# The layer-norm output of two graph-attention layers, moved from sixteen ScalarE operations to three GpSimd passes

## The chip, the cores and the metric

The kernel runs on one core of one Trainium2 chip. The metric is the device time of one execution in microseconds (us). One core has five engines that matter here, each with its own in-order queue of instructions: TensorE (PE in the profile, with its weight loads shown apart as PEld), VectorE (DVE), ScalarE (ACT), GpSimd (POOL), and SyncE (SP), which issues the DMAs.

## The reference

Four graph layers follow each other on `x` of shape 8 x 2048 x 64 (batch, nodes, features). All share one 2048 x 2048 adjacency matrix. After each layer comes a residual layer norm, cut here to what matters:

```
def _layernorm(x): m = mean(x); v = var(x); return (x - m) / sqrt(v + 1e-5)   # over 64 features
x = _layernorm(x + L0(x, adj))   # attention: softmax over neighbours, then elu; inner norm of h
x = _layernorm(x + L1(x, adj))   # attention, elu
x = _layernorm(x + L2(x, adj))   # attention, relu
x = _layernorm(x + L3(x, adj))   # a softmax per feature over the neighbours
```

Written with the statistics of a row, a norm's output is `o * rs + nm`, with `rs = 1/sqrt(var + eps)` and `nm = -mean * rs`, one value of each per node. This last step of the norms after layers 0 and 1 is what the change concerns.

## The kernel before

**Units.** A unit is one layer of one batch element. `todo` fixes their order: layer 0 of batches 0 to 3 (units 0 to 3), layer 1 of the same (4 to 7), layer 0 of batches 4 to 7 (8 to 11), layer 1 of these (12 to 15), and layer 2 of batches 0 to 7 (16 to 23). Layer 3 is a long series of matmuls that begins beside the units of layer 2 and goes on after the last one.

**Steps.** A unit has K = 16 steps, one for each block of 128 neighbours. In a step, `weights` makes a 128 x 2048 tile `w` on VectorE (maximum of a row term `r`, held in PSUM, with a column term, times the edge mask). In layer 2 only, `exponential` then takes the exponential of `w` on ScalarE. `products` multiplies `w` into the sums `acc` on TensorE. Four buffers hold `w`. At the end of a unit TensorE writes the next unit's row term `r` (`spread`, four matmuls `r<-row,ones`), which has to wait until VectorE has read the old one for the last time; VectorE then waits for the new `r`.

**Background streams.** All other work is written as Python generators which the main loop advances by one step after each step's products (`bg.step()`). `yield n` lets n steps go by before the generator's next piece is issued. So the generators and their yields set, at build time, the place of each background instruction in each engine's queue; `tc.keep_in_program_order` keeps that order. Waits on the chip are for data only: an instruction that is reached before its input is there holds its engine's queue.

**The streams around the change.** After a unit's last step a chain starts: `finish(u)` (transposes the sums, divides, adds the residual, normalizes), two steps of pause, then `scores(layer+1, b)`, which transposes the new `x` on TensorE (`p_xT...v<-ident,x`) and derives the next layer's scores. `features0(b)` prepares layer 0 of the later batches. In `finish` for layers 0 and 1:

- `side_stats` computes the row sums on GpSimd by repeated halving (`sq_x`, `st_x`), ScalarE squares the row (`sq_x<-o`), and GpSimd ends with a power (`st_x<-isw_x,mhalf`) and the two columns `rs` and `nm` (both in `st_x`).
- Line 1145: sixteen ScalarE operations, one for each block of 64 features, write `x<-o,st_x`. After each four of them comes `yield 1`.
- `xn.settle()`: a tile of `Rows` with `unit=True` keeps a column of ones in front of each row's 64 features, which overwrites the place where the last feature of the block before would lie. GpSimd first copies those last features to the end of the tile (`x<-x`, 128 x 16) and then sets the ones (`x<-`, memset). `Rows.parts` describes the resulting layout: features 0 to 62 in place, feature 63 at the end of the tile.

Others on GpSimd in these units are `hb` and `eh` (residual and elu), `pv` (values times their column factor, read by the next unit's products), `tree` (a sum over rows that TensorE reads for `p_mean`), `rT` (the row term, split in three) and `y`.

`now[1]` is the number of the unit whose steps are being issued when a line of a generator runs. A unit's `finish` lies in later units: its output is written one or two units after its last step.

Of the kernel before, what the change touches and what calls it, by code (L numbers as in the profile page):

```python
# [14 lines left out]
AF = mybir.ActivationFunctionType  # L15
ALU = mybir.AluOpType
# [34 lines left out]
def gnn4_kernel(ctx: ExitStack, tc: tile.TileContext, t, out):  # L51
# [3 lines left out]
    K = N // P  # L55
# [51 lines left out]
    class Banks:  # L107
# [4 lines left out]
        pool = None  # L112
# [28 lines left out]
    pe, dve, act, pool = (InOrder(e) for e in (nc.tensor, nc.vector, nc.scalar, nc.gpsimd))  # L141

    def psum(name):
        return pm.tile([P, 512], F32, tag="pm", name=name)

    def bc_f(v, n=K, f=F):
        return v[:, :, None].to_broadcast([P, n, f])

    def bc_k(v, n=K, f=F):
        return v[:, None, :].to_broadcast([P, n, f])  # L150
# [241 lines left out]
    for layer in range(3):  # L392
        rs = early.tile([P, F1], F32, tag="rs_w", name=f"rs_{layer}")
# [126 lines left out]
    def side_stats(y, name, st=None):  # L520

        centered = st is not None
        if not centered:
            st = small.tile([P, 2, K], F32, tag="st", name=f"st_{name}", bufs=4)
            yield from sq_slots.take()
            sq = tmp.tile([P, K, F], F32, tag="sq", name=f"sq_{name}")
            halved(st[:, 0], sq, y)
            yield 2
            act.activation(sq, y, AF.Square)
            yield 1  # L530
        else:
            sq = y
        s1, s2 = st[:, 0], st[:, 1]
        halved(s2, sq, sq)
        sq_slots.give()
        w = small.tile([P, 2, K], F32, tag="isw", name=f"isw_{name}", bufs=4)
        var, q = w[:, 0], w[:, 1]
        pool.tensor_scalar(var, s2, 1.0 / F, LN_EPS, ALU.mult, ALU.add)
        if not centered:
            pool.tensor_scalar(q, s1, 1.0 / F, None, ALU.mult)  # L540
            pool.tensor_tensor(s1, q, q, ALU.mult)
            pool.tensor_tensor(var, var, s1, ALU.subtract)
        pool.tensor_tensor(s2, var, mhalf, ALU.pow)
        if not centered:
            pool.tensor_scalar(q, q, -1.0, None, ALU.mult)
            pool.tensor_tensor(s1, q, s2, ALU.mult)
        yield 4 if now[0] < 2 else 2
        return s1, s2

    def stats(y, n, name):  # L550

        st = small.tile([P, 2, n], F32, tag="st", name=f"st_{name}", bufs=4)
        yield from sq_slots.take()
        sq = tmp.tile([P, n, F], F32, tag="sq", name=f"sq_{name}")
        act.activation(sq, y, AF.Square)
        dve.tensor_reduce(st[:, 0], y, AX.X, ALU.add)
        yield 2 if now[0] < 2 else 1
        dve.tensor_reduce(st[:, 1], sq, AX.X, ALU.add)
        sq_slots.give()
        yield from inv_std(st, n, name)  # L560
        return st[:, 0], st[:, 1]
# [490 lines left out]
    def finish(u):  # L1052
        layer, b = u.layer, u.b
        yield from oT_slots.take()
        oT = tmp.tile([P, 2, 512], F32, tag="oT", name=f"oT_{u.n}")
        for c in range(2):
            act.copy(oT[:, c], u.acc[c])
        if layer == 0:
            hb = early.tile([P, K, F], F32, tag="hb", name=f"hb_{u.n}", bufs=1)
            for sl, y in V[0, b].parts:  # L1060
                pool.tensor_tensor(
                    hb[:, :, sl], y, bc_k(gamma[:, sl], K, y.shape[2]), ALU.mult
                )
        yield 1
        yield from o_slots.take()
        o = tmp.tile([P, K, F], F32, tag="o", name=f"o_{u.n}", bufs=2)
        o5 = o.rearrange("p (c h s) f -> p c s h f", c=2, h=2)
        done = 0
        while done < 4:
            width = Banks.width()  # L1070
            ps = []
            yield from pm_slots.take(width)
            for i in range(done, min(done + width, 4)):
                c, s0 = i // 2, 2 * (i % 2)
                p = psum(f"p_o_{u.n}_{c}_{s0}")
                for s in range(2):
                    k = s0 + s
                    pe.matmul(
                        p[:, s * 2 * F1 : (s + 1) * 2 * F1],
                        lhsT=oT[:, c, k * P : (k + 1) * P],  # L1080
                        rhs=RH[layer].rearrange("p h f -> p (h f)"),
                        start=True,
                        stop=True,
                    )
                ps.append((c, s0, p))
            done += width
            if done >= 4:
                oT_slots.give()
            yield 2 if width == 2 else 1
            for c, s0, p in ps:  # L1090
                p4 = p[:, : 4 * F1].rearrange("p (s h f) -> p s h f", s=2, h=2)
                den = small.tile([P, 2, 2], F32, tag="den", name=f"den_{u.n}_{c}_{s0}")
                dve.reciprocal(den, p4[:, :, :, F])
                if layer == 2:
                    dve.tensor_tensor(
                        o5[:, c, s0 : s0 + 2],
                        p4[:, :, :, :F],
                        den[:, :, :, None].to_broadcast([P, 2, 2, F]),
                        ALU.mult,
                    )  # L1100
                    continue
                for s in range(2):
                    for h in range(2):
                        act.activation(
                            o5[:, c, s0 + s, h],
                            p4[:, s, h, :F],
                            AF.Copy,
                            scale=den[:, s, h : h + 1],
                        )
            pm_slots.give(width)  # L1110
        if layer == 2:
            for sl, x in x_cur[b].parts:
                dve.scalar_tensor_tensor(o[:, :, sl], o[:, :, sl], 0.0, x, ALU.max, ALU.add)
            yield 1
        else:
            yield 1
            if layer == 0:
                pool.tensor_tensor(o, o, hb, ALU.add)
                yield 2

            yield from e_slots.take()
            e = tmp.tile([P, K, F], F32, tag="e", name=f"eh_{u.n}")
            act.activation(e, o, AF.Relu, scale=-1.0)
            act.activation(e, e, AF.Exp, scale=-1.0)
            yield 1
            for sl, x in x_cur[b].parts:
                pool.tensor_tensor(
                    e[:, :, sl], e[:, :, sl], x, ALU.add
                )
            act.activation(o, o, AF.Relu)  # L1130
            yield 1
            pool.tensor_tensor(o, o, e, ALU.add)
            e_slots.give()
            yield 2
        if now[0] < 3:
            nm, rs = yield from side_stats(o, f"x_{u.n}")
        else:
            nm, rs = yield from stats(o, K, f"x_{u.n}")
        xn = Rows(x_cur[b].t, layer < 2)
        if layer == 2:  # L1140
            dve.tensor_tensor(o, o, bc_f(rs), ALU.mult)
            dve.tensor_tensor(xn.v, o, bc_f(nm), ALU.add)
        else:
            yield 1
            for k in range(K):
                act.activation(
                    xn.block(k), o[:, k], AF.Identity, scale=rs[:, k : k + 1], bias=nm[:, k : k + 1]
                )
                if k % 4 == 3:
                    yield 1  # L1150
            xn.settle()
        o_slots.give()
        x_cur[b] = xn
        V[layer + 1, b] = xn
        if layer < 2:
            yield 1
# [7 lines left out]
    now = [0, 0, 0]  # L1164
# [273 lines left out]
    for n, (layer, b) in enumerate(todo):  # L1438
# [10 lines left out]
        for jb in range(K):  # L1449
# [12 lines left out]
            if jb == K - 1:  # L1462
                end = [lambda u=u: finish(u)]
                if layer < 2:
                    end += [2 if now[0] < 2 else 1, lambda layer=layer, b=b: scores(layer + 1, b)]
                else:
                    end += [1, lambda b=b: l3_features(b)]
                if layer == 1 and b % NB == NB - 1:
                    end += [lambda b=b: group(b // NB)]
                bg.add(chain(*end), begun=True)  # L1470
            elif not done and jb >= 10 and ready(*nxt):
                prepare(*nxt)
                prepared.add(n + 1)
                done = True
# [524 lines left out]
```

## Time and profile before

| | |
|---|---|
| median of 3 runs | 1397.81 us (1397.5 to 1398.58) |
| profiled execution | 1401.63 us, of which span 1399.8 us |
| PE busy | 1220.0 us (87% of the span) |
| DVE busy | 1208.8 us (86%) |
| ACT busy | 821.6 us (59%) |
| POOL busy | 770.2 us (55%) |
| `x<-o,st_x` on ACT | 256 instructions, 91.5 us busy |

The span is that of the profiled execution from its first to its last instruction. Busy times count the time in which an engine has at least one instruction running; matmuls overlap each other, so a PE that shows 96% can still be waiting in part. All instructions carry the line of a helper (L80), so groups are told apart by the names of their tiles, with buffer numbers left out: `x<-o,st_x` reads `o` and `st_x` and writes `x`.

### The profile page before, as it was taken

To read this page: it belongs to the slowest core of one execution; us is meant where nothing else is said; L and a number is where in the kernel's file an instruction comes from. 1 tells how busy PE (TensorE), PEld (TensorE's weight loads), DVE (VectorE), ACT (ScalarE), POOL (GpSimd) and SP (SyncE) were. 2 spreads that over 40 slices of the span, in tenths; PEclk is the share of its full clock that TensorE was granted. 3 is DMA by queue.
4 is the path that set the end of the run, shared out by engine and by line. 5 is a ranking of instruction groups with operands and counts; after the bars stand their busy time and mean duration, and the time that the engine had idled before them with its cause. 6 is when DMAs were issued, how large, how long until landed. Compare 5 with 4: busy or idle time off the path is not lost.

```text
span 1399.8 us, 19531 instructions
## 1 busy us (share of the span) xinstructions
PE 1220.0 (87%) x7169; PEld 624.2 (45%) x7169; DVE 1208.8 (86%) x1108; ACT 821.6 (59%) x1593; POOL 770.2 (55%) x1075
## 2 busy tenths in 40 slices
PE   3699888999898988999997879799989999976995
PEld 3333233333343333333332324256645565666995
DVE  3889889999997999889998888998879798877876
ACT  3444543666646753555547996868666758664432
POOL 1666776546765663645542342443555564776664
PEclk8699999999999999999999988999999899998998
DMA  8640000000000221222101000034543444511111
GB/s 291 228 95 1 1 2 1 1 2 1 3 1 1 91 76 47 78 74 93 32 1 39 1 15 1 22 94 129 146 122 92 127 119 138 160 28 33 35 38 34
DMA packets 112010, 87.24 MB, mean 62 GB/s; under 512 B 57917, under 2 KB 90845, under 8 KB 110882
## 3 DMA queue, kind: packets, MB, share of 16 engines
q1 hardware_dynamic: 111538, 85.79, 20.9%
q8 instruction: 59, 0.97, 0.3%
q14 instruction: 45, 0.37, 0.1%
q10 hardware_dynamic: 368, 0.12, 0.0%
HBM read 60.40 MB, written 25.45 MB: 61 GB/s over the span
## 4 chain that ended last, share of the span: by engine, by line
PE 49%; DVE 24%; ACT 11%; issue 7%; POOL 6%; DMA 2%; SPq 1%; ACTq 0%; DVEq 0%; POOLq 0%
PE acc L80 26%; DVE w L80 16%; PE p_l L80 14%; ACT w L80 2%; PE p_o L80 2%; ACT x L80 2%; DVE o L80 1%; PE r L80 1%; PE p_s L80 1%; POOL sq_x L80 1%; DMA raw<-in_adjT_dram 1%; DVE nd L80 1%; POOL st_x L80 1%; DVE edge L80 1%; ACT y L80 1%
## 5 line engine op out<-in xcount | busy, mean ns | idle before, releaser
L80 DVE SCALAR_TENSOR_TENSOR w<-r,se,edge 128x2048 f32<-128x2048 f32 (+1 forms) x270 | 552.9, 2102 | 30.9 <-PE r L80 22.6
L80 PE MATMUL acc<-w,pv 128*64 128x512 f32 x2048 | 494.1, 615 | 53.0 <-DVE w L80 39.4
L80 DVE SCALAR_TENSOR_TENSOR w<-r,lo_g,edge 128x2048 f32<-128x2048 f32 (+1 forms) x144 | 297.8, 2096 | 26.0 <-PE r L80 12.4
L80 ACT ACTIVATE w<-w,down_g 128x2048 f32<-128x2048 f32 (+1 forms) x144 | 256.8, 1808 | 64.6 <-DVE w L80 57.4
L80 PEld LDWEIGHTS p_l<-v,mask 128*128 128x128 f32 x2048 | 256.3, 196 | 61.8 <-issue 48.5
L80 PE MATMUL p_l<-v,mask 128*128 128x256 f32 x2048 | 271.1, 291 | 10.6 <-POOL mask L80 7.0
L80 PE MATMUL acc<-w,x 128*64 128x512 f32 x1024 | 261.8, 640 | 19.2 <-ACT w L80 16.3
L80 PEld LDWEIGHTS acc<-w,pv 128*64 128x64 f32 x2048 | 132.6, 139 | 307.6 <-issue 182.4
L80 POOL TENSOR_TENSOR sq_x<-sq_x 128x32 f32<-128x32 f32 (+4 forms) x207 | 110.1, 532 | 63.8 <-ACT sq_x L80 49.3
L80 PEld LDWEIGHTS acc<-w,x 128*64 128x64 f32 x1024 | 66.5, 143 | 138.9 <-issue 86.6
L80 ACT ACTIVATE x<-o,st_x 128x64 f32<-128x64 f32 x256 | 91.5, 445 | 13.2 <-POOL st_x L80 13.2
L80 ACT ACTIVATE nd<-p_l,empty 128x256 f32<-128x256 f32 x64 | 30.2, 471 | 109.1 <-PE p_l L80 109.1
L80 ACT ACTIVATE o<-p_o,den 128x64 f32<-128x64 f32 x256 | 55.8, 323 | 47.0 <-DVE den L80 47.0
L80 PE MATMUL p_o<-rh,oT 128*128 128x130 f32 x384 | 61.9, 298 | 24.4 <-DVE o L80 6.7
L80 PEld LDWEIGHTS p_o<-rh,oT 128*128 128x128 f32 x384 | 50.2, 197 | 58.3 <-issue 32.3
L80 ACT COPY oT<-acc 128x512 f32<-128x512 f32 x48 | 25.7, 587 | 80.8 <-PE acc L80 80.8
L80 POOL TENSOR_TENSOR st_x<-isw_x,mhalf 128x16 f32<-128x16 f32 x24 | 70.5, 2938 | 1.9
L80 POOL TENSOR_TENSOR eh<-eh,x 128x1024 f32<-128x1024 f32 (+2 forms) x24 | 36.5, 1532 | 47.0 <-ACT eh L80 47.0
L80 DVE RECIPROCAL nd<-nd 128x256 f32<-128x256 f32 x32 | 55.7, 1742 | 0.0
L80 POOL TENSOR_TENSOR d<-x,wa_bc 128x1024 f32<-128x1024 f32 x8 | 19.0, 2379 | 66.5 <-DVE x L80 66.5
L80 POOL TENSOR_TENSOR sq_x<-o 128x512 f32<-128x512 f32 x23 | 29.3, 1273 | 34.6 <-DVE o L80 34.1
L80 ACT ACTIVATE xs<-x,nodes 128x64 f32<-128x64 f32 x128 | 44.7, 434 | 3.2 <-PE p_xT L80 3.2
(258 smaller groups left out, 1523.5 us busy)
## 6 DMA issues: line engine op xcount, KB each, us to landing
mask<-mask_d SPq DMA_DIRECT2D x132, 256.0 KB
mask_d<-mf SPq DMA_DIRECT2D x32, 512.0 KB
raw<-in_adjT_dram SPq DMA_DIRECT2D x8, 1024.0 KB
raw<-in_adjT_dram SPq DMA_DIRECT2D x16, 512.0 KB
x<-in_x_dram SPq DMA_DIRECT2D x8, 512.0 KB
x_d<-x SPq DMA_DIRECT2D x8, 512.0 KB
e<-x_d SPq DMA_DIRECT2D x64, 64.0 KB
out_dram<-o SPq DMA_DIRECT2D x64, 64.0 KB
```

Of the source, the lines that this page charges most:

```text
L80: ins = f(*args, **kwargs)
```

## The change

Where `now[1]` is 4 or more, the sixteen ScalarE operations and `settle` are replaced. GpSimd multiplies the whole 128 x 16 x 64 tile `o` by `rs`, broadcast along the features, in place; adds `nm` for the 63 features of each row that lie in place (128 x 16 x 63); adds it for the last features (128 x 16) into the end of the tile; and sets the ones. Four yields of one step each become one of two steps. Below 4 the code is as it was.

```
         else:
             yield 1
-            for k in range(K):
-                act.activation(
-                    xn.block(k), o[:, k], AF.Identity, scale=rs[:, k : k + 1], bias=nm[:, k : k + 1]
-                )
-                if k % 4 == 3:
-                    yield 1
-            xn.settle()
+            if now[1] < 4:
+                for k in range(K):
+                    act.activation(
+                        xn.block(k),
+                        o[:, k],
+                        AF.Identity,
+                        scale=rs[:, k : k + 1],
+                        bias=nm[:, k : k + 1],
+                    )
+                    if k % 4 == 3:
+                        yield 1
+                xn.settle()
+            else:
+                pool.tensor_tensor(o, o, bc_f(rs), ALU.mult)
+                for sl, x in xn.parts:
+                    pool.tensor_tensor(x, o[:, :, sl], bc_f(nm, K, x.shape[2]), ALU.add)
+                pool.memset(xn.v[:, :, 0:1], 1.0)
+                yield 2
         o_slots.give()
```

## The prediction, made before the changed kernel had run

> **What bounds the kernel now.** I began with the page's engine totals and its 40 slices, to see which engine is full where.
>
> ```profile
> PE 1220.0 (87%) x7169; PEld 624.2 (45%) x7169; DVE 1208.8 (86%) x1108; ACT 821.6 (59%) x1593; POOL 770.2 (55%) x1075
> PE   3699888999898988999997879799989999976995
> DVE  3889889999997999889998888998879798877876
> ACT  3444543666646753555547996868666758664432
> POOL 1666776546765663645542342443555564776664
> ```
>
> A slice is 35 us. DVE and PE are at 8 or 9 nearly everywhere; ACT is half busy, but reaches 9 in the two slices from 735 to 805 us. Which of these stages the change lies in needs times by unit. I take a unit's end at the last of its four `acc<-emptyT` matmuls. By that, units 4 to 7 run from 236 to 402 us, 8 to 15 to 744, unit 16 (the first of layer 2) to 792.8 and unit 17 to 845.1. The view of windows gives for these stretches, and for units 6 and 7 alone, the length and then the busy time of PE, PEld, DVE, ACT and POOL:
>
> ```profile
> 236.00:402.00 166.00, 154.88 (x782) 61.76 (x780) 154.82 (x111) 101.55 (x328) 103.73 (x159) 1.00 0.01 2
> 402.00:744.00 342.00, 311.90 (x1735) 122.46 (x1731) 317.08 (x234) 180.28 (x496) 189.51 (x279) 0.98 0.16 51
> 319.30:401.70 82.40, 77.60 (x395) 31.30 (x393) 77.61 (x58) 50.13 (x162) 60.06 (x96) 1.00 0.01 2
> 744.40:792.80 48.40, 38.16 (x180) 13.75 (x178) 39.36 (x26) 47.04 (x69) 15.89 (x25) 0.96 0.08 28
> 792.80:845.10 52.30, 41.73 (x189) 14.69 (x187) 47.35 (x48) 47.21 (x53) 17.13 (x24) 0.90 0.03 10
> ```
>
> In units 4 to 15 DVE is busy 472 of 508 us and PE 467: those two set the pace, and ACT (55%) does not. In unit 16 ACT is busy 47.04 of 48.40 us and is the bound, since every step there also takes an exponential on it. In unit 17 ACT and DVE are level at 90%. So I read the waits of DVE in both stretches (engine, what waited and for what: us in total, times, longest), first 236 to 744.4, then unit 16:
>
> ```profile
> DVE w L80 <- PE r L80: 23.0, 12, 3.2
> DVE den L80 <- PE p_o L80: 4.7, 3, 3.5
> DVE mean L80 <- ACT mean L80: 3.9, 2, 3.1
> ...
> DVE w L80 <- ACT eh L80: 2.7, 1, 2.7
> DVE w L80 <- PE r L80: 2.3, 1, 2.3
> DVE w L80 <- ACT w L80: 1.8, 1, 1.8
> DVE w L80 <- PE acc L80: 1.6, 1, 1.6
> ```
>
> In the first stretch nearly all waiting is for `r` at a unit's end; its shortest case is 1.11 us, so 13.3 of the 23.0 us are there anyhow. ACT appears with 3.9 us. The timeline of ACT says why, in unit 8: it stood 8.46 us at the first `x<-o,st_x`, and what was queued behind it (`mean`, `o`) came late to PE and DVE.
>
> ```profile
> 419.28 1.44 ACT L80 ACTIVATE x<-o,st_x 128x64 f32<-128x64 f32 x4 [8.46 <-POOL st_x L80]
> ```
>
> In unit 16, 2.7 + 1.8 + 1.6 = 6.1 us of DVE's waits come from a late ACT: the exponentials are late, so PE is late, so no `w` buffer is free.
>
> **What the Trainium skill says.** "GPSIMD Engine Reference", 3.1, gives 4497 ns for a float32 tensor_tensor add of 2048 elements per partition; half of it, 2.25 us, is an estimate for 1024. The trace agrees: 1.90 us for `pv<-x,se`, up to 2.38. The same page, 1, says that GpSimd's SBUF interfaces are shared with VectorE, with contention for DVE instructions of two SBUF inputs. `w<-r,se,edge` has one tensor in PSUM and one in SBUF, and shows none: I split it and its counterpart of layer 2, in single instructions of 128 x 2048, by overlap with POOL: the 84 with under 5% overlap and the 70 with 90% or more both average 2337 ns. "ScalarE: Activation LUTs", What ACT_TABLE_LOAD costs, gives 186 ns + 0.833 ns an element + 93 ns for each pointer operand, with 93 ns of overlap back to back: 425 ns here, or 332 in a row. The trace has 445 as the mean and 357 in a row (91.5 us / 256).
>
> **The change part by part.** The groups kept apart by shape:
>
> ```profile
> L80 ACT ACTIVATE x<-o,st_x 128x64 f32<-128x64 f32 x256 | 91.5, 445 | 13.2 <-POOL st_x L80 13.2
> L80 POOL TENSOR_TENSOR pv<-x,se 128x1024 f32<-128x1024 f32 x8 | 15.2, 1899 | 0.0
> L80 POOL TENSOR_TENSOR eh<-eh,x 128x1008 f32<-128x1008 f32 x8 | 15.9, 1993 | 33.6 <-ACT eh L80 33.6
> ```
>
> *How often.* The order of instructions of both built programs (no times) shows 32 of the 256 ScalarE operations left. `finish` lags: the outputs of units 0 and 1 are written while `now[1]` is 2 and 3, that of unit 2 in unit 4. So 14 of 16 outputs change, among them those of units 14 and 15, written in units 16 and 17.
>
> *Removed from ACT.* 14 x 16 operations, 14 x 5.7 us = 80 us busy. In units 4 to 15 this lies beside DVE and PE and is worth only the waits above. In unit 16 it is on the path.
>
> *Added to POOL.* Per output: the multiply by a broadcast column like `pv` (1.90; 2.38 at the upper end, as `d<-x,wa_bc`), the add of 1008 like `eh` (1.99; 2.34 as `hb`), 0.23 for 16 elements, less the 0.20 copy; the memset stays. That is 3.9 to 4.7 us, I take 4.2; times 14, 59 us. DVE, PE and ACT work hides it where POOL has room: 73% busy in units 6 and 7 becomes 83%.
>
> *Moved.* The passes follow `st_x` in POOL's own queue, so POOL itself waits for nothing new. Behind them come `pv`, `tree`, `rT`, `sq_x` of other streams, each later by up to 4.2 us. The next reader, PE's `p_xT...v`, comes five steps (some 12 us) after the passes are issued, two steps (4.8 us) earlier than before against `st_x`. I compared, for each of the 14 outputs, the time `st_x` was ready plus 4.5 us with the time at which PE came to a place two steps earlier: the slack is 11.8 to 34.7 us. I cost this wait at nothing; if that cover were gone, PE would stand in front of its `acc` matmuls. DMAs are the same in number; the `row` loads move with their streams.
>
> *PE's background.* Transposes just ahead of `r` (steps 13 and 14) delay it. In the new order they leave step 14 in units 7, 8 and 15 (before: 2.56, 3.05, 2.56 us of wait, after some 1.1 to 1.5: -4), and small pieces come in at units 9, 10, 12 and 13 (+1.5). PE has the same sum of work, so part of it is late elsewhere.
>
> *The sum.* Units 4 to 15: order at `r` -2.5 (of at most -9.7), the wait for `mean` -3.9, less crowding at `den` in unit 12 -0.6 (of 5.7), new waits behind a fuller POOL +3: together -4. Unit 16: ACT 47.0 - 5.8 = 41.3 us, DVE 39.4 plus 1.1 at `r`; I put the unit at 42.9, so -5.5 (between -2 and -7.9). Unit 17: DVE 47.35 busy and 5 us of waits, half of which hang on ACT: -2.5 (between 0 and -4.5). From step 11 of unit 18 on, all engines' orders are equal to before, so the rest is shifted. Sum -12. The profiled execution (1401.6 us, span 1399.8) lies 3.8 us above the median; I take the 12 us off the median: **1385.8 us**.
>
> **The rivals.**
>
> *Only layer 2 gains.* PE is 92% busy in units 4 to 15, so a transpose taken from a boundary delays another step. For it: the same PE work; against it: the 3.9 us behind the ACT wait have a cause that goes. -4 to -8: 1390 to 1394.
>
> *Nothing measurable.* In unit 16 PE and DVE are within 3 us of the relieved ACT and their mutual waits take its place: -2, 1396. Against it: 6.1 us of DVE's waits there are named.
>
> *Slower: POOL becomes the late one.* Its queue is in order, and PE waits for `pv` (slack 3.0 us at unit 7's start) and `tree` (1.5 us at 482 us). If POOL's backlog when the passes are issued exceeds the smallest slack of 11.8 us, the products PE needs come late by up to 4.2 us, once a unit: 12 x 4.2 = 50 us at most, half of it likely, less 8 from layer 2: about +17, 1415. For it: POOL's 83% in units 6 and 7; against it: in units 4 to 15 POOL stood idle for 31 us waiting for ACT's `x`, which goes.
>
> *More than planned.* All boundary waits at their floor and units 16 and 17 at DVE's own time: -9.7 - 3.9 - 7.9 - 4.5 = -26: 1372.
>
> *The change does less than it says* is excluded by the count; it does more (14 outputs, not 12).
>
> **How the numbers follow.** Forecast (-8 to -18) 0.50; only layer 2, 0.20; more than planned 0.09; nothing 0.09; slower by POOL 0.12. About 0.2% (2.8 us) is what a measurement of this kernel can tell from no change. Faster by more 0.79, within 0.09, slower 0.12. The range 1375 to 1397 takes in the bounds of units 16 and 17 and both smaller rivals, and leaves out the slower case and the end of the larger gain, together about 0.2.
>
> **What would show it.** ACT loses some 80 us busy and POOL gains some 59; POOL shows 128 x 1024 and 128 x 1008 passes of 1.9 to 2.4 us; unit 16 is near 43 us with ACT below 97%, unit 17 near 50; DVE no longer waits for `mean` in unit 8. It is wrong if PE waits for POOL's `x`, `pv` or `tree` by more than a few us, if the waits at `r` sum to over 23 us, or if unit 16 keeps its 48 us.

## The result, and the profile after

The changed kernel takes 1389.16 us in the median of 4 runs (1386.13 to 1391.82), beside 1398.19 us for the kernel before on the same chip: a ratio of 0.9934 with a 95% interval of 0.9907 to 0.9961, so 9 us faster. Run again later on another chip (19 runs), it had 0.9948 (0.9933 to 0.9964). The forecast was 1385.8 us.

The profiled execution took 1391.82 us, its span 1390.0 us, which is 9.8 us less than before. The page's engine totals and four of its rows of slices:

```profile
PE 1220.5 (88%) x7169; PEld 623.5 (45%) x7169; DVE 1214.1 (87%) x1108; ACT 751.3 (54%) x1369; POOL 817.7 (59%) x1103
...
PE   3689898999898979999997879799989899976996
...
DVE  3889889999999999889999899998879798877876
ACT  4444543446245544343436987867666768564432
POOL 1566777558668686756743543343646564676665
```

ACT lost 70.3 us and POOL gained 47.5 us. The work went where the diff says. DVE's number of instructions is the same (1108), yet it is busy 5.3 us longer: nothing in the diff touches DVE, so this is the first sign of a cost that the prediction did not have. The groups kept apart by shape:

```profile
L80 POOL TENSOR_TENSOR o<-o,st_x 128x1024 f32<-128x1024 f32 x14 | 26.6, 1900 | 0.0
L80 POOL TENSOR_TENSOR x<-o,st_x 128x1008 f32<-128x1008 f32 x14 | 26.3, 1876 | 1.1
...
L80 ACT ACTIVATE x<-o,st_x 128x64 f32<-128x64 f32 x32 | 11.6, 448 | 2.1 <-POOL st_x L80 2.1
...
L80 POOL TENSOR_TENSOR x<-o,st_x 128x16 f32<-128x16 f32 x14 | 3.3, 234 | 0.0
```

Fourteen outputs changed, and one costs 1.90 + 1.88 + 0.23 = 4.0 us of POOL. The view of windows for the stretches that were shown of before (units 4 to 7, 8 to 15, 6 and 7, 16, 17; length, then busy time of PE, PEld, DVE, ACT, POOL):

```profile
235.30:404.70 169.40, 156.73 (x772) 61.16 (x770) 159.36 (x110) 78.89 (x253) 110.00 (x152) 0.98 0.01 2
404.70:741.40 336.70, 311.73 (x1750) 122.12 (x1748) 315.25 (x235) 141.88 (x381) 229.72 (x313) 0.98 0.16 51
321.30:404.70 83.40, 77.44 (x379) 29.63 (x377) 78.71 (x56) 37.83 (x115) 57.44 (x83) 0.98 0.01 2
741.40:786.70 45.30, 36.25 (x184) 13.71 (x182) 40.43 (x27) 43.12 (x52) 17.62 (x27) 1.00 0.09 30
786.70:838.40 51.70, 41.37 (x189) 15.42 (x187) 47.98 (x56) 41.86 (x37) 19.96 (x26) 0.87 0.03 10
```

Measured by the exact ends of the units (the table further down), units 4 to 7 became 3.7 us longer, units 8 to 15 5.9 us shorter, unit 16 3.1 us and unit 17 0.6 us shorter. Unit 18, for which no gain was expected, lost 2.7 us (57.5 to 54.8), which is about what DVE's two waits for `den` there became shorter (1.96 + 1.85 us before, 0.54 + 0.41 after). DVE's waits (us in total, times, longest) in units 4 to 15, and then in unit 16:

```profile
DVE w L80 <- PE r L80: 23.4, 12, 2.8
DVE den L80 <- PE p_o L80: 3.0, 3, 1.8
DVE s_top L80 <- ACT s L80: 2.8, 2, 1.9
...
DVE w L80 <- PE acc L80: 3.5, 3, 1.7
DVE w L80 <- PE r L80: 1.3, 1, 1.3
```

The 3.9 us behind ACT's `mean` are gone. The waits for `r` did not shrink: 23.4 us against 23.0. What DVE lost instead is not in this view at all, since the profile counts it as busy. I looked for it by comparing each small DVE instruction with the shortest of its own kind, and found instructions of 0.2 us that last up to 2.3 us. The timeline of unit 5 (start, duration, engine, operation) has one:

```profile
288.29 0.20 DVE L80 TENSOR_TENSOR s<-h,st_h 128x32 f32<-128x32 f32 x1
288.31 2.08 POOL L80 TENSOR_TENSOR x<-o,st_x 128x1008 f32<-128x1008 f32 x2
288.53 1.74 DVE L80 TENSOR_TENSOR s<-s,s_off 128x32 f32<-128x32 f32 x1
...
290.30 0.43 ACT L80 ACTIVATE se<-s 128x16 f32<-128x16 f32 x3 [6.09 <-DVE s L80]
290.30 0.19 DVE L80 TENSOR_REDUCE s_top<-s 128x1 f32<-128x32 f32 x1
```

`s<-h,st_h` began just before the new pass and took 0.20 us. `s<-s,s_off`, of the same size, began after it and ended only when the pass over 1008 elements had (the timeline shows it with the short one behind it; alone it ran to 290.21). ACT, which needs `s` for `se`, stood 6.09 us; some 1.5 of these are the hold. Such excess over the shortest of a kind, counted where it is more than 0.25 us, sums to 15.2 us before and 20.3 us after between 236 and 845 us; of the latter 5.4 us lie under the new passes.

### The profile page after: what moved, and what is told of

It is laid out like the page before. It is cut to its first block, busy times and chain, and to the rows that moved or that the text cites. A ratio compares the mean times of both kernels' runs of the same rounds, so it can differ in the third digit from the quotient of the medians.

```text
span 1390.0 us, 19341 instructions
## 1 busy us (share of the span) xinstructions
PE 1220.5 (88%) x7169; PEld 623.5 (45%) x7169; DVE 1214.1 (87%) x1108; ACT 751.3 (54%) x1369; POOL 817.7 (59%) x1103
## 4 chain that ended last, share of the span: by engine, by line
PE 29%; DVE 15%; ACT 5%; issue 4%; POOL 2%; POOLq 0%; DVEq 0%; ACTq 0%
PE p_l L80 14%; PE acc L80 12%; DVE w L80 8%; DVE o L80 2%; ACT w L80 1%; PE p_o L80 1%; DVE nd L80 1%; DVE x L80 1%; ACT sp L80 1%; DVE fs L80 1%; PE r L80 1%; POOL sq_x L80 1%; POOL st_x L80 0%; PE p_s L80 0%; ACT L80 0%
## 5 line engine op out<-in xcount | busy, mean ns | idle before, releaser
L80 PE MATMUL acc<-w,x 128*64 128x512 f32 x1024 | 259.1, 637 | 14.5 <-ACT w L80 10.8
L80 POOL CAST mask<-edge 128x2048 fp32r<-128x2048 fp8e4 x16 | 30.5, 1906 | 24.1 <-PE p_l L80 24.1
```

Of the source, the lines that this page charges most:

```text
L80: ins = f(*args, **kwargs)
```

## The experiments

The table collects what the texts below speak of. A unit is taken to end where its last `acc<-emptyT` starts; lengths in us are from one profiled execution of each kernel, and two of the changed kernel differ by up to 0.9 us in these three stretches. What lies outside of them differs more between executions: units 0 to 3 took 235.7 us in one profile of the changed kernel and 238.7 in the other, and all that is behind unit 18 takes 490 to 497 us over the fourteen profiles. A profiled execution can also lie off its kernel's median, by 2.7 us above it for the changed kernel and 7.3 below it for e7. So the lengths tell where something changed, the ratios how much. "Held" is the excess of the small DVE instructions between 236 and 845 us. The ratio is to the kernel before on the same chip.

| kernel | units 4-7 | 8-15 | 16-18 | held | ratio (95%) |
|---|---|---|---|---|---|
| before | 165.7 | 342.6 | 158.1 | 15.2 | 1 |
| changed | 169.4 | 336.7 | 151.8 | 20.3 | 0.9934 (0.9907 to 0.9961) |
| e1_late_only | 165.7 | 342.4 | 150.8 | 16.2 | 0.9961 (0.9937 to 0.9985) |
| e2_early_only | 169.4 | 337.7 | 158.2 | 20.7 | 0.9982 (0.9968 to 0.9997) |
| e3_order_only | 181.8 | 337.1 | 159.7 | 12.1 | 1.0073 (1.0050 to 1.0096) |
| e4_work_only | 166.8 | 342.5 | 153.4 | 26.0 | 0.9988 (0.9977 to 1.0000) |
| e5_triple_add | 173.5 | 340.1 | 154.1 | 26.7 | 1.0010 (0.9996 to 1.0024) |
| e6_mean_pool | 163.9 | 328.6 | 152.3 | 10.4 | 0.9851 (0.9830 to 0.9872) |
| e7_before_mean_pool | 165.9 | 337.5 | 155.3 | 6.2 | 0.9986 (0.9973 to 0.9999) |
| e8_late_order | 166.9 | 337.7 | 150.8 | 18.6 | 0.9938 (0.9918 to 0.9959) |
| e10_mean_pool_late | 164.7 | 331.4 | 150.6 | 6.0 | 0.9886 (0.9868 to 0.9904) |
| e11_mean_reduce | 164.1 | 337.1 | 150.6 | 9.0 | 0.9906 (0.9882 to 0.9930) |
| e12_mean_triple | 169.1 | 332.9 | 152.2 | 12.8 | 0.9910 (0.9896 to 0.9924) |

### The change taken apart by place: e1 and e2

Only the outputs that are written in layer 2 (units 16 and 17) change:

```
-            if now[1] < 4:
+            if now[1] < 16:
```

> GpSimd writes only the outputs of units 14 and 15, those that are issued in units 16 and 17; the other fourteen stay on ScalarE, and the order of all engines up to unit 16 is that of before. Theory (the gain is ScalarE's relief in the first units of layer 2): units 16 to 18 shrink by 6 us as in the changed kernel (48.4, 52.3, 57.5 to about 45, 52, 55) and the time is 5 to 7 us under before, ratio about 0.9955. Rival (the gain is made in units 4 to 15): within 2 us of before.

1390.8 us beside 1396.97. Units 16 to 18 are 7.3 us shorter, units 4 to 15 are as before.

Only the twelve outputs before layer 2 change:

```
-            if now[1] < 4:
+            if now[1] < 4 or now[1] >= 16:
```

> GpSimd writes the twelve outputs issued in units 4 to 15; those of units 14 and 15 stay on ScalarE. Theory: units 4 to 15 take some 506 us instead of 508 as in the changed kernel, units 16 to 18 keep their 158 us: 2 to 3 us under before, ratio about 0.998. Rival (gain made in units 4 to 15): 7 to 9 us under before, ratio 0.994.

1394.93 us beside 1396.97. Units 4 to 7 lose 3.7 us and units 8 to 15 gain 4.9. The two parts, 0.39% and 0.18%, make 0.57% together, and the whole 0.66% and 0.52% in its two measurements: they add up within their intervals. Two outputs of fourteen bring about two thirds of the gain.

### The change taken apart by kind: e3 and e4

The order of the changed kernel with the old work: the sixteen ScalarE operations and `settle` are issued in one go, so that TensorE and VectorE have the changed kernel's order.

```
-                pool.tensor_tensor(o, o, bc_f(rs), ALU.mult)
-                for sl, x in xn.parts:
-                    pool.tensor_tensor(x, o[:, :, sl], bc_f(nm, K, x.shape[2]), ALU.add)
-                pool.memset(xn.v[:, :, 0:1], 1.0)
+                for k in range(K):
+                    act.activation(xn.block(k), o[:, k], AF.Identity, ...)
+                xn.settle()
                 yield 2
```

> All outputs stay on ScalarE, but the sixteen operations of an output are issued in one go and followed by a pause of two steps, as the GpSimd passes of the changed kernel are: the orders on TensorE and VectorE are those of the changed kernel. Theory (the work's place gives the gain, the order about nothing): within 3 us of before in units 4 to 15, and units 16 to 18 not faster, or slower, since the ScalarE burst is denser there: 0 to +5 us. Rival (the two steps fewer and the other order give the gain): 5 to 9 us under before.

1408.46 us beside 1396.97, 0.73% or 10 us slower, where 0 to 5 were expected. Units 6 and 7 lose 17 us. The timeline there, POOL, DVE, ACT and PE (idle time and its releaser in brackets):

```profile
345.18 0.21 POOL L80 COPY x<-x 128x16 f32<-128x16 f32 x1 [12.64 <-ACT x L80]
...
352.51 1.88 DVE L80 TENSOR_TENSOR s<-h,st_h 128x32 f32<-128x32 f32 x1 [4.06 <-POOL st_h L80]
...
356.65 0.38 PE L80 MATMUL p_r<-ident,se 128*16 128x128 f32 x1 [6.21 <-ACT se L80]
...
386.82 5.41 ACT L80 ACTIVATE x<-o,st_x 128x64 f32<-128x64 f32 x16 [9.79 <-POOL st_x L80]
...
393.08 1.97 PE L80 MATMUL p_xT<-ident,xs 128*128 128x128 f32 x8 [6.70 <-ACT o L80]
```

POOL stands 12.64 us at `settle`'s copy with `st_h` queued behind it, so DVE waits for `st_h` and PE for `se`; 40 us later ACT stands 9.79 us at its first operation and `o` comes late. Thus, with the new order, ACT's in-order queue is what the passes relieve in these units. Against the kernel before they gain nothing there (units 6 and 7: 83.4 us, before 82.4). In units 8 to 15, though, this kernel gains 5.5 us with no work moved, while e4 below, with the work moved and the old order, stays at 342.5 us: the gain there is one of order.

The work of the changed kernel with the old order:

```
-                yield 2
+                yield 4
```

> The GpSimd passes of the changed kernel, but with a pause of four steps behind them: the orders on TensorE and VectorE are those of before. Theory: the head-of-line wait of ScalarE in unit 8 and the ScalarE work of units 16 to 18 are gone while the transposes stay where they were ahead of r: 8 to 12 us under before, ratio 0.992 to 0.994, the same as the changed kernel or a little better. Rival (order gives the gain): within 3 us of before.

1394.43 us beside 1396.97: missed, since 8 to 12 us of gain were expected and 2.5 came (1.7 by the ratio, whose interval reaches 1.0000). Units 16 to 18 keep 4.7 us. In units 4 to 15 nothing is left. The wait of 3.9 us behind `mean` is gone and unit 8 is 4.1 us shorter, but DVE is held 26.0 us instead of 15.2, and unit 13 is 4.5 us longer. Unit 13 has the longest hold of a small instruction in all traces:

```profile
652.74 4.37 DVE L80 SCALAR_TENSOR_TENSOR mean<-mean,later,mean 128x64 f32<-128x64 bf16 x1
652.84 1.89 POOL L80 TENSOR_TENSOR pv<-x,se 128x1024 f32<-128x1024 f32 x1
...
654.70 2.33 POOL L80 TENSOR_TENSOR o<-o,eh 128x1024 f32<-128x1024 f32 x1
...
657.10 1.25 POOL L80 TENSOR_TENSOR sq_x<-o 128x512 f32<-128x512 f32 x1
```

The two passes follow each other without a gap, and an instruction of 0.25 us when free ended only after the second. The same one took 1.00 us in the kernel before; up to it, this execution lies 2.1 us ahead of that one. The 3.4 us that it is held longer here are more than this whole lead.

### More on POOL: e5

```
-                for sl, x in xn.parts:
-                    pool.tensor_tensor(x, o[:, :, sl], bc_f(nm, K, x.shape[2]), ALU.add)
+                for _ in range(3):
+                    for sl, x in xn.parts:
+                        pool.tensor_tensor(x, o[:, :, sl], bc_f(nm, K, x.shape[2]), ALU.add)
```

> The changed kernel with the two adds of an output issued three times (the same values are written again): 14 x 3.9 = 55 us more on GpSimd, every order else the same. Theory of the prediction (slack of 11.8 us covers GpSimd): 0 to +2 us against the changed kernel, so ratio to before 0.993 to 0.995. New theory (a small VectorE operation with two SBUF inputs stands still while a GpSimd pass runs; the 53 us of new passes cost VectorE 5.4 us in the profile): +4 to +7 us against the changed kernel, ratio 0.996 to 0.999, with more slow `mean` and `s` operations. Rival (GpSimd late for PE): +15 us or more, with PE or ScalarE waiting for GpSimd's x.

1397.51 us beside 1395.52, which by the ratios (1.0010 against 0.9934 and 0.9948) is 0.6 to 0.8%, 9 to 11 us, above the changed kernel: more than the 4 to 7 us of the new theory, less than the rival's 15. So the cover of POOL's work is not whole: 56 us more of the same passes cost. The held time grew by 6.4 us; e12 below shows that holding is not the only cost.

### The held operations taken off VectorE: e6, e7, e11

The longest held kind is the correction of `mean`, 48 operations of 0.25 us when free. Here GpSimd does it, in two; the orders of TensorE and SyncE are those of the changed kernel. ScalarE's order is not: since `yield 1` became `yield 3`, its casts of `mean` behind each correction stand two steps later in its queue. This goes for e7, e10, e11 and e12 too, and no run has this shift alone:

```
-            dve.scalar_tensor_tensor(m, a, later[:, i : i + 1], m, ALU.mult, ALU.add)
-            yield 1
+            mt = small.tile([P, F], F32, tag="mt", name=f"mt_{n}_{i}", bufs=1)
+            pool.tensor_tensor(mt, a, later[:, i : i + 1].to_broadcast([P, F]), ALU.mult)
+            pool.tensor_tensor(m, m, mt, ALU.add)
+            yield 3
```

> The changed kernel, with the correction of `mean` (two for each of the 24 units, on VectorE with two SBUF inputs, up to 2.1 us each under a GpSimd pass) done on GpSimd in two small operations instead, so that GpSimd's own queue orders it behind the passes. Theory (VectorE bounds units 4 to 15 and its standing still under GpSimd passes counts): VectorE loses 20 us of busy time there, and the kernel is 8 to 14 us under the changed one, ratio to before 0.983 to 0.988. Rival (PE, 93% busy, takes its place, or the pieces come late from GpSimd's queue and hold ScalarE): within 3 us of the changed kernel or slower.

1373.1 us beside 1395.52, and faster than both other kernels: its interval (0.9830 to 0.9872) lies wholly below the changed kernel's. The engine totals of its page:

```profile
PE 1215.0 (89%) x7169; PEld 625.1 (46%) x7169; DVE 1193.1 (87%) x1060; ACT 752.5 (55%) x1369; POOL 854.4 (62%) x1199
```

DVE has 21 us less, where 48 free operations would be 12; POOL has 37 more. Units 4 to 15 are 13.6 us shorter. The same edit on the kernel before:

> The kernel before with the same edit of `mean` alone. Theory: VectorE loses 18.7 us of busy time in units 4 to 15 and 3.9 us of waits for ScalarE: 8 to 14 us under before, ratio 0.990 to 0.994. Rival: within 3 us of before or slower.

1393.76 us beside 1395.52: missed. Its DVE is relieved just as well (held 6.2 us), but ACT's queue is still the crowded one. In unit 8 a timeline of ACT and DVE shows

```profile
417.41 0.24 ACT L80 CAST mean<-mean 128x64 bf16<-128x64 f32 x1 [10.57 <-POOL mean L80]
...
426.75 0.18 DVE L80 RECIPROCAL den<-p_o 128x4 f32<-128x4 f32 x1 [6.49 <-ACT mean L80]
```

The correction stands in POOL's queue behind a chain for `st_x` that ends at 416.7; ACT waits 10.57 us for it with `xs`, `x` and `o` behind, and DVE waits 6.49. Unit 8 is 48.6 us long here, 39.1 in e6. The profiled execution (1386.45 us) lies at the low end of its 22 runs (1386.45 to 1400.22), so its unit lengths show more gain than the kernel has; why the runs scatter so is left open.

To separate the operation's own time from the hold, each one that had left DVE was replaced by a reduction of the same tile, which has one input:

```
+            mx = small.tile([P, 1], F32, tag="mx", name=f"mx_{n}_{i}", bufs=1)
+            dve.tensor_reduce(mx, m, AX.X, ALU.max)
             mt = small.tile([P, F], F32, tag="mt", name=f"mt_{n}_{i}", bufs=1)
```

> The mean correction is on GpSimd, and in the place of each of the 48 VectorE operations stands a VectorE reduction of the same 128x64 tile, which has one input and whose output nobody reads. So VectorE has nearly the old number of operations (48 of some 0.2 us, 8 to 10 us), and the orders of TensorE, ScalarE and GpSimd are those of the kernel with the correction on GpSimd. Standstill theory: an operation of one input is never held, so only its own time comes back: 1375 to 1383 us, no reduction longer than 0.3 us. Rival, VectorE's number of operations in the chain of w is what counts and the standstill costs nothing: back to the changed kernel's time, 1386 to 1390.

1383.0 us beside 1396.81. The tile's view (shortest, median, longest in ns):

```profile
L80 DVE TENSOR_REDUCE mx<-mean x48: 187/209/220, 60.7 to 837.9; 128x1 f32<-128x64 f32 x48
...
  POOL mean L80: 42.9, 14
```

No reduction is held: the longest takes 220 ns, though twelve of those between 236 and 845 us began under a GpSimd instruction of over 1 us. The time lies between both: 0.55% above e6, for 9.9 us of DVE work and a wait that I had not meant to add (the last line of the view: GpSimd, which overwrites `m`, waits for the reduction that reads it, 42.9 us in all), and 0.42% below the changed kernel on the same chip (0.9948; 0.9933 to 0.9964), with an interval that just clears that one and overlaps that of its first measurement. A reduction is 0.04 us shorter than the free operation, 2 us in all; so some 4 us remain (about 0 to 8 by the two intervals, an estimate) that point to the hold or to the later casts on ScalarE, which e11 has as well; the added wait may hide more. That the hold exists is shown by the instructions. Its share of the 12 to 14 us (by the ratios) that e6 gains on the changed kernel is not settled.

### Cover again, and spacing: e12, e8, e10

e6 with the additions issued three times:

> The correction on GpSimd and the two additions of nm issued three times (only the last counts), so that GpSimd has some 55 us more. With the correction on VectorE the same doubling of work cost about 8 us. Standstill theory: most of what was held is no longer on VectorE, so it costs 1 to 5 us more than with single additions: 1374 to 1378. Cover theory: GpSimd's own lateness was the cost; it has 12 more us here, so at least the same 8 us come: 1381 to 1388.

1384.88 us: 0.6% above e6 (0.9910 and 0.9851), the cover theory's figure. Here DVE is hardly held more (12.8 against 10.4 us), so the cost is another one. It sits first in unit 6 (41.4 us in e6, 47.3 here); POOL, DVE and PE there:

```profile
335.26 6.10 POOL L80 TENSOR_TENSOR x<-o,st_x 128x1008 f32<-128x1008 f32 x6
...
345.38 2.93 POOL L80 TENSOR_TENSOR st_h<-isw_h,mhalf 128x16 f32<-128x16 f32 x1
...
348.35 1.88 DVE L80 TENSOR_TENSOR s<-h,st_h 128x32 f32<-128x32 f32 x1 [2.91 <-POOL st_h L80]
...
352.48 0.28 PE L80 MATMUL p_r<-ident,se 128*16 128x128 f32 x1 [5.06 <-ACT se L80]
```

`st_h` comes late behind the passes, then `s`, `se` and PE. Units 8 to 15 are 4.3 us longer too; where was not traced. So a late POOL costs as well, once the passes are long; in the changed kernel, between 236 and 845 us, DVE has no wait for `st_h`, and PE's waits for `se` are 1.5 us at the longest.

The old spacing of four steps where the output is issued before unit 8, on the changed kernel (e8) and on e6 (e10):

```
-                yield 2
+                yield 4 if now[1] < 8 else 2
```

> The changed kernel, but with a pause of four steps behind the passes while now[1] is under 8, two steps later on: the order of before in units 4 to 7, something near the changed one in units 8 to 15. Theory (the shorter pause gains in units 8 to 15 and loses in 4 to 7): units 4 to 7 take 167 us instead of 169, units 8 to 15 some 337: 2 to 3 us under the changed kernel, ratio 0.991. Rival (each order is a throw of its own, its gain not tied to the stretch): anywhere from 0.992 to 1.000.

> The changed kernel with the mean correction on GpSimd and, in the outputs issued before unit 8, the old spacing of four steps. If the order of the early units and the standstill of VectorE are separate costs, the 1 to 2 us that the spacing gave alone come on top of the 1373: 1369 to 1373 us. If the early spacing only moved where VectorE met a GpSimd pass, nothing is left to gain: 1372 to 1376.

1387.46 us beside 1395.52 for e8, which its interval does not tell from the changed kernel: units 4 to 7 win 2.5 us back, unit 8 loses 1.8. That is the rival's range, not the 0.991 of the theory. 1379.98 us beside 1396.81 for e10, above both expected ranges, so not better than e6: unit 8 takes 45.4 us instead of 39.1. The changed kernel, run again, stands beside these:

> The changed kernel again, to stand beside the others on the same chip. Every theory: 1386 to 1391 us, a ratio near 0.994 to the kernel before.

1389.79 us beside 1396.81. The best version that ran is e6.

## Why the prediction was right, and where it was wrong

The direction, most of the part of layer 2 and the order of size held; the way through units 4 to 15 did not. That their sum came near the forecast is luck, since its terms failed one by one.

**Count and cost of the passes.** Fourteen outputs, 79.9 us off ACT's group (91.5 to 11.6), as forecast. ACT's 5.7 us an output came from the trace (357 ns in a row); the 425 and 332 ns beside it are estimates. POOL's 4.2 us an output were 4.0. Both engine totals moved less than their groups (70.3 and 47.5 us), mainly because busy times are unions of overlapping instructions. POOL did not become fuller in units 6 and 7: 83% of the time was forecast, and it is busy 57.44 of 83.40 us, 69%, as other pieces of its work moved away (96 instructions there became 83). The prediction also misread the slices: ACT's two 9s are the 23rd and 24th, 770 to 840 us, not 735 to 805. Nothing rests on it, since the windows by unit are right.

**Layer 2.** Unit 16 was to lose 5.5 us and lost 3.1; unit 17 was to lose 2.5 and lost 0.6, since DVE alone is busy 47.98 of its 51.7 us. Unit 18, counted as only shifted because its orders are equal from step 11 on, lost 2.7. So 8.0 us were forecast and 6.3 came, 3.7 of them in the two units that were named and 2.7 in one that was not. ACT in unit 16 is at 95% (43.12 of 45.30 us), inside the bound that was named.

**The order at `r`.** -2.5 us: failed. The cases at units 7, 8 and 15 shrank, others grew, and the sum went from 23.0 to 23.4 us, over the 23 us that the prediction had named as a sign of being wrong. That TensorE's same work is late elsewhere was named as the reason against; it took all. The order did help in units 8 to 15 (e3, 5.5 us), but not at `r`, where I had put it.

**The wait behind `mean`.** -3.9 us: it disappeared as read, and with it unit 8 became 4.1 us shorter in e4. But there the holds grew by 10.8 us and nothing was left at the end of unit 15. Ending a wait of DVE is no gain where other delays follow in the same chain. The term for `den` in unit 12, -0.6, came out larger: DVE's waits for `den` in units 4 to 15 fell by 1.7 us.

**The cost on VectorE.** This is the step that failed: "shows none". I had tested contention on `w` alone, whose two inputs are one in PSUM and one in SBUF, and which is indeed free (2337 ns). The small operations with both inputs in SBUF were not tested, though the page that I had cited ("GPSIMD Engine Reference", 1) names just that condition. They stood in the trace of before: `mean<-mean,later,mean` averaged 493 ns there, twice its shortest. So did a control for `w` itself: the steps of the first unit take the row term from SBUF, not PSUM, and average 2526 ns.

```profile
L80 DVE SCALAR_TENSOR_TENSOR w<-r,se,edge 128x2048 f32<-128x2048 f32 x210 | 480.8, 2338 | 0.0
...
L80 DVE SCALAR_TENSOR_TENSOR w<-row,se,edge 128x2048 f32<-128x2048 f32 x16 | 39.9, 2526 | 0.0
...
L80 DVE SCALAR_TENSOR_TENSOR mean<-mean,later,mean 128x64 f32<-128x64 bf16 x48 | 23.6, 493 | 6.2 <-ACT mean L80 6.2
```

The "+3" for a fuller POOL was put on waits for POOL's products, of which there were none. In their place DVE was held 5.1 us more, and 10.8 us more with the old order (e4). How much of that the whole kernel pays is not settled (e11).

**The sum.** In these profiles units 4 to 15 gave 2.2 us for a forecast of 4, layer 2 gave 6.3 for 8; the rest differs by 1.3 us, as much as two executions of one kernel do. The 2.2 us are 3.7 lost in units 4 to 7 and 5.9 gained in units 8 to 15, which e3 and e4 put down to the order. The rival in which only layer 2 gains (4 to 8 us) was close: the first measurement, 9 us, lies just outside its range, and the second, 0.52% or 7 us, inside it. e2's 0.18% speaks against its strict form.

**The slower rival.** POOL had room for its 47.5 us, but not for much more: e5 and e12 put 0.6 to 0.8% on 56 us. The slack to PE's `p_xT...v` was the right thing to check for that one reader, but too narrow: the reader that fails first in e12 is `s`, through `st_h`.

## What to carry to other kernels

Before work goes to GpSimd beside a busy VectorE, split every kind of small VectorE instruction by whether it starts under a GpSimd pass, not the long ones only: here those with two SBUF inputs waited until the pass ended, once until a second one had, and the profile books this as busy time. A mean far above the shortest case of the same shape is the sign. And where a named wait goes, ask what is next in the same chain before counting it: here one of 3.9 us went and other delays took its place, while two of fourteen moved outputs, written where layer 2 loads ScalarE, brought about two thirds of the gain.

## What the runs showed of the hardware

The Trainium skill, "SBUF — State Buffer", Who interferes with whom, says that VectorE and GpSimd share a port pair, that a VectorE instruction with two SBUF inputs contends with a GpSimd instruction that reads SBUF, that the one issued later stands still for the whole of the other, and that one with at most one SBUF input does not contend, outside the two-port modes. I split the small VectorE instructions of fourteen traces (before, after and the twelve runs), between 236 and 845 us, by whether they began under a GpSimd instruction of over 1 us that had over 0.1 us to go ("under a pass"), or no GpSimd instruction ran beside them ("free"):

| VectorE instruction | inputs | free, mean ns | under a pass |
|---|---|---|---|
| `s<-s,s_off` 128x32 | two, SBUF | 192 | 15 of 15 held, mean 1799 |
| `beyond<-beyond,far_g` 128x1 | two, SBUF | 159 | 14 of 14 held, mean 1815 |
| `den<-p_o` 128x4 | one, PSUM | 166 | none of 248 held, mean 166 |
| `s_top<-s` 128x32 | one, SBUF | 179 | none of 34 held, mean 184 |
| `sc_g<-sc_g` 128x4, tensor_scalar | one, SBUF | 160 | 10 of 10 held, mean 1613 |

These rows agree with the page. A held instruction of the table ends 0.01 to 0.09 us after the GpSimd instruction. The last row is of one input and held all the same, which fits the page's exception for two-port modes; no run shows the mode itself. What I had not expected is how much this is for so little work: a 0.2 us instruction took up to 2.3 us under one pass and, once, 4.37 us under two in a row (e4), with the next `w` behind it. The large `w` shows the same split: with the row term in SBUF, 28 of 28 (two in each trace) that began under such a pass with over 0.4 us to go took 3.36 to 4.00 us; with it in PSUM, none of 731 took over 2.35. Nor do all GpSimd instructions hold. Of the VectorE instructions of 0.2 us with two SBUF inputs (nine kinds, named by `mean`, `s`, `beyond`, `s_g`, `sc_g` and `tt_g`) that began under a GpSimd pass over 512 or more elements with over 0.4 us to go, 193 of 193 in whole traces were held, 97 of them `mean<-mean,later,mean`; under the 2.9 us of the power (`st_x<-isw_x,mhalf`, `st_h<-isw_h,mhalf`, 128x16) none of 30 was. Its inputs lie in SBUF too, so here the page's rule goes further than what was measured.
